# An attention-and-FFN block in float32: queries and keys turned by VectorE and moved through DRAM, with a longer look-ahead

## The chip, the cores and the metric

The kernel runs on one core of a Trainium2 chip. The metric is device time in microseconds (us) of one execution, the median of several runs. A profile is taken from one further execution. TensorE is PE in the profile, VectorE DVE, ScalarE ACT, GpSimd POOL, SyncE SP.

## The reference

One transformer block, B = 8 batches of S = 128 tokens, width 512, everything in float32. Two residual steps:

```python
x = x + attn(cond(x, W[adapter_ids]), wq, wk, wv, wo)          # 32 heads of 16, causal
x = x + ffn(cond2(x, ...), gate, kernel, bias, lora_A, lora_B, ...)

# cond2: attention over a paged cache, 32 query heads, 8 key/value heads of 128
q = rope(rmsnorm(x @ Wq.T, q_norm_w), pos)     # pos = cache_seqlens + arange(128)
k = rope(rmsnorm(x @ Wk.T, k_norm_w), pos);  v = x @ Wv.T
k_all = concat([k_cache[block_table], k])      # 512 cached keys + 128 own keys
v_all = concat([v_cache[block_table], v])
o = softmax(where(valid, q @ k_all.T / sqrt(128), -1e30)) @ v_all
y = o @ Wo.T
# ffn: y @ kernel + bias + two low-rank (LoRA) terms
```

Each key/value head serves four query heads.

## The kernel before

**Phase one** (lines 276 to 798, about the first 220 us) does the first attention, batch by batch, and prepares what the second needs: the cos/sin tables (`tables`, on GpSimd), the gathered adapter weights `cw`, and the merged FFN weights (`merge_loads`, `merge_gates`, `merge_a`, `merge_b`, `merge_w`). x after the first step is kept in SBUF transposed (`x1T`) and in DRAM (`x1_kept`).

**Phase two** is a loop over 64 units, `u = 0 .. 64`. A unit is one key/value head with its four query heads (`g`) and one batch (`b`). Units run in pairs: two neighbouring heads of the same batch, whose cached keys and values lie beside each other and are gathered together. Batches run inside pairs of heads, so that the last pair of heads is units 48 to 63. What pass `u` of the loop issues, in program order:

- `scores(u)`: for each of four heads, one matmul of the head's queries `qT` (the stationary operand) against 512 cached keys `kT`, one against 128 own keys `kTo`; a VectorE step (line 902) that adds the mask and takes the row maximum; an exponential and a division on ScalarE. Score buffers in PSUM (`p_sc`) are two, so the third head waits until the first head's VectorE step is done. Between the heads, `between(r)` issues the query projection of the next unit (`q_matmul`, 4 x 128x512). At the third head `pair_keys(u)` stands.
- After the heads, `q_turn` (rotary embedding of the next unit's queries: three VectorE multiplications, one GpSimd addition, squares on ScalarE), then four VectorE transposes of the probabilities (line 883) and 16 transfers `pT<-fl` on SP's queue, which exchange 32-row blocks so that whole 128x128 transposes result. `pT` is used in the next pass.
- the next unit's key/value projection (`kv_matmul`, `kv_turn`);
- `values(u - 1)`: probabilities of the unit before times values (`op`, line 963), copied to `oT` by VectorE;
- `norms(u + 1)`: the RMS norm factors (power on GpSimd, line 244);
- `queries(u + 1)`: four TensorE transposes of the turned queries `qa` (line 254), evicted to `qT` by ScalarE;
- `out_proj(u - 1)`: `yp` (line 982), added to `y_acc[b]` by VectorE (line 989);
- `own_keys(u + 1)`: one TensorE transpose of the own keys (line 271), evicted to `kTo`.

The cached keys of units 0 to 3 are turned by TensorE (`keys`, line 263). From unit 4 on `turn_keys` turns the keys of a pair in 32x32 blocks by VectorE (line 840), and 16 transfers `kT<-flk` (`move_keys`, line 853), eight in each of two passes, put the blocks in their places inside SBUF. All of these, the weight loads (`load_qkv`, `load_wo`) and the FFN's loads stand in order on SP's queue; the gathers stand on GpSimd's.

The FFN of a batch (`ffn_flip`, `ffn_lora`, `ffn`) runs one pass after the batch's last output projection: passes 51, 53, ... 63, and 64 for the last batch, which has an order of its own (`flips_last`, `out_proj_turned`).

`tile_a` is one ring of twelve 128x512 buffers shared by both phases (`cw`, `la`, `lb`, `sq`, `qa`, `qb`, `qT`, `oT` and others). Tables `ca`, `sa` for all batches lie in SBUF throughout. The order of the work is written out by hand (`tc.manual_schedule()`): each engine takes its instructions in program order.

Of the kernel before, what the change touches and what calls it, by code (L numbers as in the profile page):

```python
# [19 lines left out]
P = 128  # L20
# [21 lines left out]
def block_kernel(  # L42
# [47 lines left out]
    def tile_a(shape, name):  # L90
        return both.tile(shape, F32, tag="a", name=name, bufs=12)
# [18 lines left out]
    ca = [one([P, B, D2], F32, f"ca_{n}") for n in range(2)]  # L110
    sa = [one([P, B, D2], F32, f"sa_{n}") for n in range(2)]
# [11 lines left out]

    weights = {}

    def load_qkv(g):
        wq = wpool.tile([P, KC, REP * D2], F32, tag="wq", name=f"wq_{g}")
        wkv = wpool.tile([P, KC, 2 * D2], F32, tag="wkv", name=f"wkv_{g}")
        e = slice(g * REP * D2, (g + 1) * REP * D2)
        nc.sync.dma_start(out=wq[:], in_=wq2[:, e].rearrange("(c p) e -> p c e", p=P))  # L130
        nc.sync.dma_start(out=wkv[:], in_=wkv2[:, g, :].rearrange("(c p) e -> p c e", p=P))
        weights[g] = [wq, wkv]

    def load_wo(g):
        wo = wpool.tile([P, REP, DM], F32, tag="wo", name=f"wo_{g}")
        e = slice(g * REP * D2, (g + 1) * REP * D2)
        nc.sync.dma_start(out=wo[:], in_=wo2[e, :].rearrange("(r p) o -> p r o", p=P))
        weights[g].append(wo)
# [46 lines left out]
    def q_turn(u):  # L185

        b = units[u][1]
        s = st[u]
        qp = s["qp"]

        def table(t, cols):
            return t[:, b, cols].unsqueeze(1).to_broadcast([P, REP, cols.stop - cols.start])
# [6 lines left out]
        def turn():  # L199
            nc.vector.tensor_tensor(qa[:], qp[:], table(ca[0], slice(0, D2)), ALU.mult)  # L200
            nc.vector.tensor_tensor(qb[:, :, lo], qp[:, :, hi], table(sa[0], lo), ALU.mult)
            nc.vector.tensor_tensor(qb[:, :, hi], qp[:, :, lo], table(sa[0], hi), ALU.mult)
# [18 lines left out]
    def kv_turn(u):  # L221

        b = units[u][1]
        s = st[u]
        kp, ss = s["kp"], s["ss"]
        junk = both.tile([P, D2], F32, tag="junk", name=f"junk_{u}", bufs=1)
        nc.scalar.activation(junk[:], kp[:, :D2], AF.Square, accum_out=ss[:, REP:])
        vo = both.tile([P, D2], F32, tag="vo", name=f"vo_{u}", bufs=3)
        nc.scalar.copy(vo[:], kp[:, D2:])
        ka = both.tile([P, D2], F32, tag="ka", name=f"ka_{u}")  # L230
        kb = both.tile([P, D2], F32, tag="kb", name=f"kb_{u}")
        nc.vector.tensor_tensor(ka[:], kp[:, :D2], ca[1][:, b, :], ALU.mult)
        nc.vector.tensor_tensor(kb[:, lo], kp[:, hi], sa[1][:, b, lo], ALU.mult)
        nc.vector.tensor_tensor(kb[:, hi], kp[:, lo], sa[1][:, b, hi], ALU.mult)
# [3 lines left out]
    def norms(u):  # L238
# [6 lines left out]
        nq = both.tile([P, REP], F32, tag="nq", name=f"nq_{u}", bufs=3)  # L245
# [3 lines left out]

    def queries(u):  # L250
        s = st[u]
        tp = p_tp.tile([P, REP, S], F32, tag="tp", name=f"qTp_{u}")
        for r in range(REP):
            nc.tensor.transpose(tp[:, r, :], s["qa"][:, r, :], ident[:])  # L254
        s["qT"] = tile_a([P, REP, S], f"qT_{u}")
        nc.scalar.copy(s["qT"][:], tp[:])  # L256

    def keys(u):

        s = st[u]  # L260
        tp = p_tp.tile([P, NBLK, P], F32, tag="tp", name=f"kgTp_{u}")
        for c in range(NBLK):
            nc.tensor.transpose(tp[:, c, :], cached(u, "kg", c), ident[:])
        kT = tile_a([P, NBLK * 4, 32], f"kT_{u}")
        nc.scalar.copy(kT[:].rearrange("p k j -> p (k j)"), tp[:].rearrange("p c k -> p (c k)"))
        s["kT"] = kT[:]

    def own_keys(u):
        s = st[u]
        tp = p_tp.tile([P, S], F32, tag="tp", name=f"kTp_{u}")  # L270
        nc.tensor.transpose(tp[:], s["ka"][:], ident[:])
        s["kTo"] = both.tile([P, S], F32, tag="kTo", name=f"kTo_{u}")
        nc.scalar.copy(s["kTo"][:], tp[:])  # L273


    with (
# [69 lines left out]
        ahead = both.tile([P, 4, P], I32, tag="a", name="ahead", bufs=12)  # L346
# [62 lines left out]

        def tables(n):  # L410
            for here, there in ((lo, hi), (hi, lo)):
                w_here = wn[n][:, here].unsqueeze(1).to_broadcast([P, B, HALF])
                w_there = wn[n][:, there].unsqueeze(1).to_broadcast([P, B, HALF])
                nc.gpsimd.tensor_tensor(ca[n][:, :, here], trig["cos"], w_here, ALU.mult)
                nc.gpsimd.tensor_tensor(sa[n][:, :, here], trig["sin"], w_there, ALU.mult)
            nc.gpsimd.tensor_scalar(sa[n][:, :, lo], sa[n][:, :, lo], -1.0, None, ALU.mult)
# [3 lines left out]
        def merge_loads():  # L420
# [7 lines left out]
            for key, src in (("las", lora_as), ("lbs", lora_bs)):  # L428
                merge[key] = tile_a([RANK, DM], key)
# [8 lines left out]
        def merge_gates():  # L438
# [5 lines left out]
            gs = [tile_a([P, 2, B * RANK], f"gs_{n}") for n in range(2)]  # L444
# [256 lines left out]
        for k in range(2 * B + 1):  # L701
# [4 lines left out]
            if hb == 0:  # L706
# [11 lines left out]
                if k == 2 * B:  # L718
                    queries(0)
# [27 lines left out]
            else:  # L747
# [36 lines left out]
                elif b == 2:  # L784
                    tables(1)
                    nc.gpsimd.memset(minus_half[:], -0.5)
# [8 lines left out]
        keys(0)  # L795
        own_keys(0)
# [37 lines left out]
    def turn_keys(n):  # L834


        flk = p2.tile([P, 4, NBLK, 2, 32], F32, tag="flk", name=f"flk_{n}", bufs=1)
        for h, half in enumerate(pairs[n]["kg"]):
            for m in range(2):
                nc.vector.transpose(  # L840
                    flk[:, :, 2 * h : 2 * h + 2, m, :].rearrange("p b c i -> p c b i"),
                    half[:, :, m, :],
                )
        pairs[n]["flk"] = flk
        kT = p2.tile([P, NBLK, 4, 2, 32], F32, tag="kT2", name=f"kT2_{n}")
        pairs[n]["kT"] = kT
        for m in range(2):
            st[2 * n + m]["kT"] = kT[:, :, :, m, :].rearrange("p c a i -> p (c a) i")

    def move_keys(n, a):  # L850

        for b in range(4):
            nc.sync.dma_start(
# [348 lines left out]
```

## Time and profile before

| | us |
|---|---|
| median of 3 runs | 1420.79 (1420.76 to 1423.76) |
| the profiled execution, its time | 1423.96 |
| the profiled execution, its span | 1421.1 |
| granted TensorE clock over the span | 0.997 of full |

| stretch, us from the start of the span | PE busy | DVE busy | ACT busy | POOL busy | DMA share |
|---|---|---|---|---|---|
| 14.78 to 220.69 (phase one) | 197.47 | 137.01 | 104.65 | 109.92 | 0.33 |
| 220.69 to 277.78 (units 0 to 2) | 53.55 | 34.65 | 27.37 | 23.23 | 0.40 |
| 277.78 to 1379.67 (units 3 to 62) | 1100.13 | 738.79 | 512.23 | 423.00 | 0.48 |
| 1379.67 to 1421.10 (end) | 34.20 | 11.63 | 9.81 | 1.26 | 0.15 |

A float32 matmul appears as two matmul records. The ends of matmuls are modelled, so that neighbouring records overlap; the distance from start to start is the better measure of what one costs. "Idle before" in a row is the time in which the engine had nothing to do before this instruction, and the name behind the arrow is what ended it. A `DMA_DIRECT2D` row on SPq is the issue of transfers, not their landing.

### The profile page before, as it was taken

The numbers are of one execution on the slowest core, as the hardware profiler recorded it, in microseconds if no ns is written. First come the engines' busy times: TensorE is split into PE (matmuls) and PEld (weight loads), VectorE is DVE, ScalarE is ACT, GpSimd is POOL, SyncE is SP. The second block draws the span as 40 slices with busy tenths as digits, with TensorE's granted clock in tenths as the row PEclk, the third lists the DMA queues.
The fourth block names the chain that finished last, engine by engine and source line by source line (L and its number), as shares of the span: only waits on it lengthen the run. The fifth ranks groups of instructions, "written<-read, shape, count | busy, mean of one in ns | idle before, by whom it ended". The sixth has DMA issues, their size and how long they took to land.

```text
span 1421.1 us, 20290 instructions
## 1 busy us (share of the span) xinstructions
PE 1391.5 (98%) x6244; PEld 898.5 (63%) x6244; DVE 931.8 (66%) x2266; ACT 655.9 (46%) x1520; POOL 568.2 (40%) x553
## 2 busy tenths in 40 slices
PE   6999989999999999999999999999999999999998
PEld 6877755566666666666666666666666665666555
DVE  5777846566666666666666666666666665666651
ACT  3555535444444444444444444444444444344431
POOL 5774342433333333333333333333333433343220
PEclk9999999999999999999999999999999999999999
DMA  6255013444444565444445654444456544444440
GB/s 198 75 164 183 31 37 104 129 117 118 119 115 119 161 193 151 119 119 119 119 119 159 196 148 119 118 119 119 121 160 192 152 117 136 131 111 112 115 111 30
DMA packets 156202, 180.26 MB, mean 127 GB/s; under 512 B 92416, under 2 KB 97792, under 8 KB 156096
## 3 DMA queue, kind: packets, MB, share of 16 engines
q1 hardware_dynamic: 140544, 134.39, 34.0%
q0 software_dynamic: 15552, 44.58, 10.8%
q8 instruction: 50, 0.82, 0.2%
q14 instruction: 56, 0.46, 0.1%
HBM read 75.83 MB, written 4.72 MB: 57 GB/s over the span
## 4 chain that ended last, share of the span: by engine, by line
PE 93%; DVE 2%; issue 2%; DMA 1%; ACT 1%; POOL 1%; SPq 1%; another core or an unknown queue 0%; DVEq 0%; POOLq 0%; ACTq 0%
PE op L963 19%; PE qp L177 15%; PE sc L889 15%; PE yp L982 15%; PE kvp L217 7%; PE sc L896 4%; PE fp L1044 2%; PE hp L514 2%; PE qTp L254 2%; PE pT1p L638 2%; PE qp L530 2%; PE att L673 2%; PE o L657 1%; PE sc L595 1%; PE kvp L545 1%
## 5 line engine op out<-in xcount | busy, mean ns | idle before, releaser
L902 DVE CUSTOM_DVE_ANT_0 pr<-sc,mask,nq 128x640 f32<-128x640 f32 x256 | 226.0, 884 | 144.2 <-PE sc L896 90.9
L912 ACT ACTIVATE pr<-pr,nm 128x640 f32<-128x640 f32 x256 | 211.8, 827 | 189.3 <-DVE nm L902 102.1
L889 PE MATMUL sc<-kT,qT 128*128 128x512 f32 x512 | 262.0, 593 | 0.0
L177 PE MATMUL qp<-wq,x1T 128*128 128x512 f32 x512 | 251.2, 593 | 0.0
L963 PE MATMUL op<-pT,vg 128*128 128x256 f32 x1024 | 242.0, 379 | 1.6 <-DMA pT<-fl 1.6
L203 POOL TENSOR_TENSOR qa<-qa,qb 128x512 f32<-128x512 f32 x64 | 81.8, 1278 | 375.2 <-DVE sums L879 375.2
L982 PE MATMUL yp<-wo,oT 128*128 128x512 f32 x504 | 229.2, 598 | 2.0 <-DVE oT L971 2.0
L963 PEld LDWEIGHTS op<-pT,vg 128*128 128x128 f32 x1024 | 193.9, 190 | 27.8 <-DVE sums L879 1.8
L880 ACT ACTIVATE pr<-pr,sums 128x640 f32<-128x640 f32 x256 | 208.4, 814 | 0.0
L883 DVE STREAM_TRANSPOSE fl<-pr 128x640 f32<-128x640 f32 x252 | 189.2, 808 | 0.0
L896 PEld LDWEIGHTS sc<-kTo,qT 128*128 128x128 f32 x512 | 96.4, 190 | 124.4 <-issue 119.2
L982 PEld LDWEIGHTS yp<-wo,oT 128*128 128x128 f32 x504 | 91.4, 191 | 95.1 <-issue 91.5
L160 POOL DMA_INDIRECT kg<-in_k_cache_dram,idx_kv x128 | 131.6, 1029 | 35.3 <-issue 34.8
L160 POOL DMA_INDIRECT vg<-in_v_cache_dram,idx_kv x128 | 128.6, 1005 | 37.8 <-issue 33.6
L889 PEld LDWEIGHTS sc<-kT,qT 128*128 128x128 f32 x512 | 87.7, 191 | 80.2 <-issue 77.8
L256 ACT COPY qT<-qTp 128x512 f32<-128x512 f32 x64 | 37.5, 586 | 205.3 <-PE qTp L254 204.7
L217 PEld LDWEIGHTS kvp<-wkv,x1T 128*128 128x128 f32 x512 | 97.3, 190 | 40.5 <-issue 30.1
L217 PE MATMUL kvp<-wkv,x1T 128*128 128x256 f32 x512 | 121.0, 379 | 0.0
L244 POOL TENSOR_TENSOR rs<-ss,minus_half 128x5 f32<-128x5 f32 x64 | 76.5, 1196 | 83.1 <-DVE ss L242 82.2
L177 PEld LDWEIGHTS qp<-wq,x1T 128*128 128x128 f32 x512 | 82.8, 191 | 31.5 <-issue 31.5
L896 PE MATMUL sc<-kTo,qT 128*128 128x128 f32 x512 | 99.2, 275 | 0.0
L273 ACT COPY kTo<-kTp 128x128 f32<-128x128 f32 x64 | 17.1, 267 | 166.4 <-issue 115.2
(155 smaller groups left out, 1701.1 us busy)
## 6 DMA issues: line engine op xcount, KB each, us to landing
pT<-fl SPq DMA_DIRECT2D x1008, 80.0 KB
kT<-flk SPq DMA_DIRECT2D x480, 32.0 KB
wq<-in_wq_dram SPq DMA_DIRECT2D x8, 1024.0 KB
wo<-in_wo_dram SPq DMA_DIRECT2D x8, 1024.0 KB
wkv<-in_wkv_dram SPq DMA_DIRECT2D x8, 512.0 KB
kg<-in_k_cache_dram,idx_kv POOLq DMA_INDIRECT x128
vg<-in_v_cache_dram,idx_kv POOLq DMA_INDIRECT x128
res<-x_kept SPq DMA_DIRECT2D x8, 256.0 KB
```

What stands on the lines that cost most here:

```text
L160: nc.gpsimd.indirect_dma_start(out=dst[:, c].rearrange("p n d -> p (n d)"), out_offset=None, in_=src, in_offset=bass.IndirectOffsetOnAxis( ...
L177: nc.tensor.matmul(s["qp"][:].rearrange("p h d -> p (h d)"), x1T[b][:, c, :], weights[g][0][:, c, :], start=(c == 0), stop=(c == KC - 1),)
L203: nc.gpsimd.tensor_tensor(qa[:], qa[:], qb[:], ALU.add)
L217: nc.tensor.matmul(s["kp"][:], x1T[b][:, c, :], weights[g][1][:, c, :], start=(c == 0), stop=(c == KC - 1))
L880: nc.scalar.activation(prs[r][:], prs[r][:], AF.Copy, scale=sums[:, r : r + 1])
L883: nc.vector.transpose(s["flips"][:, :, :, r, :].rearrange("p b c j -> p c b j"), prs[r][:])
L889: nc.tensor.matmul(sc[:, : NBLK * P].rearrange("p (k j) -> p k j", j=32), s["qT"][:, r, :], s["kT"], start=True, stop=True,)
L896: nc.tensor.matmul(sc[:, NBLK * P : NK], s["qT"][:, r, :], s["kTo"][:], start=True, stop=True)
L902: nc.vector.tensor_tensor_reduce(out=pr[:], in0=sc[:, :NK], in1=mask[:], scale=s["nq"][:, r : r + 1], scalar=3.0e38, op0=ALU.add, op1=ALU.min,
L912: nc.scalar.activation(pr[:], pr[:], AF.Exp, bias=nm[:, r : r + 1], scale=-1.0, accum_out=sums[:, r : r + 1],)
L963: nc.tensor.matmul(ops[h][:, : 2 * S], cached(u, "vg", c) if c < NBLK else s["vo"][:], s["pT"][:, :, c, 2 * h : 2 * h + 2, :].rearrange("p ...
L982: nc.tensor.matmul(yp[:], s["oT"][:, r, :], weights[g][2][:, r, :], start=(r == 0), stop=(r == REP - 1))
```

## The change

Seven things change together.

1. *Turning.* From unit 8 on neither queries nor own keys are transposed by TensorE. `turn_ahead(v)` turns both of a unit in 32x32 blocks by VectorE, the queries of a pair's two units interleaved element by element (`flq[..., m]`). Units 1 to 7 keep TensorE transposes (`flip`, `flip_own`), and TensorE turns the cached keys of units 0 to 7 (`flip_keys`); `turn_keys` starts at pass 5 with pair 4.
2. *Moving.* The 16 SBUF-to-SBUF transfers of a pair are replaced by five stores to DRAM in an even pass (`keys_out`) and eight loads in the odd pass after it (`keys_in`), which carry cached keys, own keys and queries.
3. *Reading.* Queries are read by the score matmuls from a tile of the pair with a step of two elements, keys from a tile in the order block, unit, chunk.
4. *Look-ahead.* The projections run 2, then 3, then 4 units ahead: pass 0 projects units 1 and 2, passes 1 to 3 one unit each, passes 4 and 5 two each, every later pass unit `u + 4`. Passes 60 to 62 have none.
5. *Tables.* The cos/sin tables go to DRAM once (`tab_kept`) and are loaded for each pair (`load_tab`).
6. *Queues.* The weights of heads 2 to 7 are issued on GpSimd's queue, the query and key/value weights three passes earlier.
7. *FFNs.* Batches 0 to 2 keep passes 51, 53, 55; batches 3 to 7 stand at passes 60 to 64.

Buffers: the `tile_a` ring shrinks from twelve to nine, some small tiles get more, and `las`, `lbs`, `gs` get tiles of their own.

```diff
 def tile_a(shape, name):
-    return both.tile(shape, F32, tag="a", name=name, bufs=12)
+    return both.tile(shape, F32, tag="a", name=name, bufs=9)
...
+def load_tab(n):
+    if n < N // 2:
+        tabs[n] = both.tile([P, 4, D2], F32, tag="tab", name=f"tab_{n}")
+        nc.sync.dma_start(out=tabs[n][:], in_=tab_kept[n % B])
...
-    nc.sync.dma_start(out=wq[:], in_=wq2[:, e].rearrange("(c p) e -> p c e", p=P))
+    queue = nc.sync if g < 2 else nc.gpsimd
+    queue.dma_start(out=wq[:], in_=wq2[:, e].rearrange("(c p) e -> p c e", p=P))
...
 def turn_keys(n):
-    flk = p2.tile([P, 4, NBLK, 2, 32], F32, tag="flk", name=f"flk_{n}", bufs=1)
+    flk = p2.tile([P, 4, 2, NBLK + 1, 32], F32, tag="flk", name=f"flk_{n}", bufs=1)
     # four nc.vector.transpose, 128x256 each, as before
+    flq = p2.tile([P, 4, REP, 32, 2], F32, tag="flq", name=f"flq_{n}", bufs=1)
+    pairs[n]["fl"] = [flk, flq]
+    turned_tiles(n)
+
+def turned_tiles(n):
+    kT = p2.tile([P, 4, 2, NBLK + 1, 32], F32, tag="kT2", name=f"kT2_{n}")
+    qT = p2.tile([P, REP, 4, 32, 2], F32, tag="qT2", name=f"qT2_{n}")
+    pairs[n]["to"] = [kT, qT]
+    for m in range(2) if n else (1,):
+        s = st[2 * n + m]
+        s["kT"] = kT[:, :, m, :NBLK].rearrange("p a c i -> p c a i")
+        s["qT"] = [qT[:, r].rearrange("p a i m -> p (a i) m")[:, :, m] for r in range(REP)]
+        s["kTo"] = kT[:, :, m, NBLK]
...
+def turn_ahead(v):
+    (flk, flq), m = pairs[v // 2]["fl"], v % 2
+    nc.vector.transpose(
+        flq[:, :, :, :, m].rearrange("p b r i -> p r b i"),
+        st[v]["qa"][:].rearrange("p r d -> p (r d)"),
+    )
+    nc.vector.transpose(flk[:, :, m, NBLK], st[v]["ka"][:])
+
+def keys_out(n):
+    flk, flq = pairs[n]["fl"]
+    kk = dram.tile([P, 4, 320], F32, tag="kk", name=f"k_kept_{n}", bufs=2)
+    kq = dram.tile([32, 4 * REP, 4, 64], F32, tag="kq", name=f"q_kept_{n}", bufs=2)
+    nc.sync.dma_start(out=kk[:], in_=flk[:].rearrange("p b m c i -> p b (m c i)"))
+    for a in range(4):
+        nc.sync.dma_start(
+            out=kq[:, :, a],
+            in_=flq[32 * a : 32 * a + 32].rearrange("p b r i m -> p (b r) (i m)"),
+        )
+    pairs[n]["dr"] = [kk, kq]
+
+def keys_in(n):
+    kT, qT = pairs[n]["to"]
+    kk, kq = pairs[n]["dr"]
     for b in range(4):
+        part = slice(32 * b, 32 * b + 32)
+        nc.sync.dma_start(
+            out=kT[part].rearrange("p a m c i -> p a (m c i)"),
+            in_=kk[:].rearrange("(a j) b x -> j b a x", j=32)[:, b],
+        )
+        nc.sync.dma_start(
+            out=qT[part].rearrange("p r a i m -> p (r a i m)"),
+            in_=kq[:, REP * b : REP * b + REP].rearrange("j r a x -> j (r a x)"),
+        )
 def pair_keys(u):
-    if u == 2:
-        turn_keys(u)
-    if 1 < u < N - 2:
-        for a in range(u % 2 * 2, u % 2 * 2 + 2):
-            move_keys(u // 2 + 1, a)
+    if 5 < u < N - 2:
+        if u % 2 == 0:
+            turn_ahead(u + 3)
+            keys_out(u // 2 + 1)
+        else:
+            keys_in(u // 2 + 1)
...
-pending = []
+ffn_at = {N - 13 + 2 * b: b for b in range(3)}
+ffn_at.update({N - 7 + b: b for b in range(3, B)})
 for u in range(N + 1):
+    if u < 4:
+        ahead = [u + 2] if u else [1, 2]
+    elif u < 6:
+        ahead = [2 * u - 2, 2 * u - 1]
+    else:
+        ahead = [u + 4] if u + 4 < N else []
+    early = {0: [1], 1: [2, 3], 2: [4], 3: [5], 4: [6], 5: [7]}.get(u, [])
...
-        norms(u + 1)
-        queries(u + 1)
-        for v in {0: (1,), 1: (2, 3)}.get(u, ()):
-            keys(v)
-        if u > 2 and u % 2 and u // 2 + 2 < N // 2:
-            turn_keys(u // 2 + 2)
+    if ahead:
+        norms(ahead[0])
+    for v in {0: [1], 1: [2, 3], 2: [4, 5], 4: [6, 7]}.get(u, []):
+        flip_keys(v)
+    for v in early:
+        flip(v)
+    if u > 4 and u % 2 and u // 2 + 2 < N // 2:
+        turn_keys(u // 2 + 2)
+        turn_ahead(u + 3)
...
-    if nxt:
-        own_keys(u + 1)
+    for v in early:
+        flip_own(v)
+    if len(ahead) > 1:
+        project(ahead[1])
+        norms(ahead[1])
+    if u in (0, 1, 3, 4) or u > 4 and u % 2:
+        load_tab({0: 2, 1: 3, 3: 4, 4: 5}.get(u, (u + 7) // 2))
```

`project(v)` issues `q_matmul`, `q_turn`, `kv_matmul` and `kv_turn` of one unit in a row. In phase one `load_tab(0)` and `load_tab(1)` follow the store of the tables on SP's queue.

## The prediction

> **What bounds the kernel now.** I read the page first, then the chain of waits for two loop passes in mid-kernel (u = 26 and 27), then the timeline of all engines over the same stretch, then the SP queue, then TensorE's own waits.
>
> The page: the last column that matters is PE's share of the span.
>
> ```profile
> span 1421.1 us, 20290 instructions
> PE 1391.5 (98%) x6244; PEld 898.5 (63%) x6244; DVE 931.8 (66%) x2266; ACT 655.9 (46%) x1520; POOL 568.2 (40%) x553
> ```
>
> A busy PE need not be PE at its peak, so the chain of waits decides (start us, us, what):
>
> ```profile
> 713.58 1.73 PE kvp L217 x8
> 715.31 4.32 PE op L963 x20
> 719.63 0.44 PE qTp L254 x4
> 720.06 3.44 PE yp L982 x8
> 723.50 0.11 PE kTp L271
> 723.61 0.86 PE sc L889 x2
> 724.47 0.22 PE sc L896 x2
> ```
>
> There is no wait in it: each piece starts where the last ended. A pass is 4 heads x (0.86 + 0.22) + qp 3.44 + kvp 1.73 + op 4.32 + qTp 0.44 + yp 3.44 + kTp 0.11 = 17.8 us, and the chain shows passes of 17.8 us. TensorE work that leaves a pass shortens it, until another engine's loop is longer.
>
> VectorE at the turn of a pass, and the SP queue (rows of the timeline):
>
> ```profile
> 722.01 1.42 DVE L840 STREAM_TRANSPOSE flk<-kg 128x256 f32<-128x256 f32 x4
> 723.54 0.69 DVE L989 TENSOR_TENSOR y<-yp,y 128x512 f32<-128x512 f32 x1
> 724.14 0.55 DVE L874 TENSOR_SCALAR mask<-place,lens_f 128x640 f32<-128x640 f32 x1
> 724.83 0.88 DVE L902 CUSTOM_DVE_ANT_0 pr<-sc,mask,nq 128x640 f32<-128x640 f32 x1
> 726.47 1.02 PE L889 MATMUL sc<-kT,qT 128*128 128x512 f32 x2
> ```
>
> ```profile
> 710.38 5.15 SPq L853 DMA_DIRECT2D kT<-flk  x8
> 718.03 10.89 SPq L936 DMA_DIRECT2D pT<-fl  x16
> 729.03 5.15 SPq L853 DMA_DIRECT2D kT<-flk  x8
> ```
>
> VectorE runs without a break from 722.01 into the new pass. The third head's score matmul (726.47) needs a score buffer that the first head's softmax step (L902, 724.83) gives back after some 0.95 us; 0.7 us are spare. SP issues for 16 of 17.8 us, 0.6 us a transfer. The last pT piece lands about 2.1 us after its issue (the chain near the end: "DMA pT<-fl" 2.12), at 731.0, and op wants it at 732.9.
>
> TensorE's few losses lie at the ends:
>
> ```profile
> PE yp L982 <- DVE oT L971: 2.0, 1, 2.0
> PE op L963 <- DMA pT<-fl: 1.6, 1, 1.6
> ```
>
> and in pass u = 2, where VectorE turns the first cached keys in mid-scores (windows, one pass each; PEclk third from the end):
>
> ```profile
> 705.66:723.45 17.79, 17.79 (x68) 11.23 (x67) 13.08 (x34) 8.42 (x18) 7.10 (x8) 1.00 0.44 118
> 255.89:277.78 21.89, 19.89 (x68) 11.77 (x67) 11.49 (x32) 8.79 (x19) 11.00 (x12) 0.92 0.43 122
> ```
>
> **The change part by part**, summed against this profiled execution (1423.96 us, its span 1421.1).
>
> *TensorE transposes of 56 units go.* 0.44 + 0.11 = 0.55 us each: -30.8 us. The evictions on ScalarE go too (0.59 + 0.27 a unit); it is 46% busy, nothing. Cached keys of units 4 to 7 are now turned by TensorE: 16 x 0.11 = +1.8.
>
> *VectorE takes them.* One 128x512 and one 128x128 transpose a unit. The trace has 4 of 128x640 in 3.00 us (0.75 each) and 4 of 128x256 in 1.42 (0.34): by that slope 0.61 and 0.2, 0.82 a unit. The 128x512 one writes every second element, of which there is no row: bounds are the same price and double it; I take the same. In even passes it stands between the third and fourth head, where the rows before L902 are 0.97 us idle: hidden, and what exceeds the gap has another 0.7 us before qa. In odd passes it follows the four flk transposes, ahead of y and mask. In the frame of the rows above PE's new pass starts at 722.90; VectorE ends flk at 723.35, the new transposes at 724.17, y at 724.8, mask at 725.3; L902 from 725.3 gives the buffer back at 726.25, while PE is there at 725.92. 0.33 us of stall; counted for 27 odd passes, +8.9. The bounds: nothing if the y addition is less late than I have it, 0.95 each if the strided write doubles (+26).
>
> *The move through DRAM.* Per pair of units SP issued 16 kT pieces; now it is 5 stores, 8 loads and a table load, 14, at 0.6 us: SP has no more to do than before. The stores wait for VectorE's transposes in the even pass (done some 6.2 us into it); behind them on SP stands pT, whose source is ready 12.3 us in: 5 x 0.6 fits, even 5 x 1.38 (w_eff's issue, the longest row of a plain load) is 0.8 us late only. The loads wait for stores issued a pass earlier; they end about 10.3 us into the odd pass, 1.2 MB at the 200 to 240 GB/s of busy microseconds take 5 to 6, and they are needed at 17.2. Hidden; if they came 3 us late it would be 28 x 3 us. Traffic rises from 118 GB/s to some 190. A rule speaks against it: "DMA: Bandwidth & Descriptors" in the Trainium skill (Specifications) has transfers under 512 B pay a read-modify-write, and 2048 runs a pair are 256 B, now into DRAM. The row: kT's 256-B runs, alone on the engines from 712 to 717, moved 231 KB in a summed share of 1.0 us x 16, so 18 ns a run. By the row the stores take 2.3 us of 16 engines a pair, at four times that 9 us of 34.5: the mean share goes to 0.6 or to 0.8, off the path either way. I take nothing.
>
> *Queries read with a step of two.* Each qT stationary is now every second element of a tile shared by two units. No row has a strided weight load. Contiguous ones follow each other at 0.11 us (two in 0.30), which the 0.11 us of a 128-column pass (L896, 0.22 for two) just covers. At half rate four loads in the kTo passes and one between heads 0 and 1 stick out by 0.107 each, 0.53 us a unit. The skill's "SBUF — State Buffer" (Door 1, SBUF cachelines) says that a 16-byte line needs two hits for full bandwidth; a step of 8 bytes has two. By the rule the cost is 0, by the pessimistic reading 63 x 0.53 = 33 us. I take 0.
>
> *Look-ahead in steps.* Passes 0, 4 and 5 project a second unit at their end, 5.17 us of PE work that passes 60 to 62 no longer have: no sum. But its VectorE, ScalarE and GpSimd tail (qa 0.69, 0.41, 0.41, squares 0.60, pow 1.20, mask 0.55) now stands ahead of the next L902: about 3.8 us from the last projection matmul to L902, 4.75 to its buffer, against 3.0 us of PE work: 1.75 us stall, three times, +5.3. Nothing to 3.5 each: in the u = 2 window a 2-us gap also dropped the clock to 0.92. Several PSUM evictions in a row in passes 1 to 4: +1.
>
> *Pass 2 turns nothing in mid-scores:* 21.89 - 17.79 = -4.1.
>
> *Weights on GpSimd's queue.* 18 issues at 0.8 us (wq_sb and wo_sb there: 0.83, 0.80). Queued behind are the next gathers and the qa addition, which has a whole pass to spare now. Nothing; without that cover 14 us spread over 12 passes.
>
> *Phase one.* Nine buffers in place of twelve make three lb loads wait for the last cw (155.4), so w_eff and gc leave behind them: gc lands near 163, where gs ran from 161.6 to 164.5 (mostly blocked). +0.5, at most 5. The table's 2-MB store and two loads stand on SP between xs (101) and the next xs (122.9): hidden.
>
> *Tail.* Passes 60 to 62 have 5.2 us FFN in place of 5.2 us projection, but the projection lay ahead of op and the FFN lies behind it. pT of unit 59 lands 12.3 + 10.1 + 2.1 = 24.5 us after its pass began; op is reached after 17.2 + 4.3 + 0.44 = 22.0. 2.5 lost, and an estimated 1.9 over the next three; today's 1.6 and some 0.4 go. +2.4.
>
> Sum: -30.8 + 1.8 + 8.9 + 5.3 + 1.0 - 4.1 + 0.5 + 2.4 = **-15.0**. The profiled execution would be 1409; the median of the three runs lies 3.2 us lower, so **1406**.
>
> **The rivals.** (1) *Nothing sticks out:* VectorE's odd-pass delay and the projection stalls are absorbed. For it: my slack is 0.3 us in a chain of ten instructions. Against: VectorE is back to back there today. -15.0 - 8.9 - 3 = 1394. (2) *The strided stationary operand:* weight loads at half rate. -15 + 33: **1439, slower**. It decides above 0.05 us per load (15 us over 63 x 5 loads), a pitch of 0.16 for 0.11. Against it is the line rule; for it only that no row shows one. (3) *pT comes late:* its slack falls from 1.9 to about 1.4 us as the pass shrinks, and the engines carry 60% more. Landing 0.25 us beyond it in every pass eats all (60 x 0.25 = 15): 1421; a microsecond, 1466. Against: stores and loads are issued outside pT's own 10 us. (4) *VectorE's strided transpose at double price:* -15 + 17 = 1423. That the transposes don't leave TensorE can be excluded from the diff.
>
> **How the numbers follow.** A measurement here can tell about 0.2% (2.8 us) from no change. My forecast 0.60; (1) 0.14; (2) 0.08; (3) 0.12, half of it near no change or a little under; (4) 0.06. Faster: 0.60 + 0.14, with a little of (3) and (4): 0.75. Same: 0.06. Slower: 0.19. The range from 1393, the end of (1), to 1427, past (4) and the mild half of (3).
>
> **What would show it.** PE instructions 6244 - 280 + 16 = 5980. Passes of 17.25 us when even, near 17.6 when odd, with TensorE waiting for L902 ahead of the third head. In the windows of passes 4, 5 and 6 a stall of about 2 us. Weight loads of the scores still at 190 ns, two in 0.30. pT's wait on PE only at pass 60 and later. I am wrong if op waits for pT in mid-kernel, if score weight loads lengthen, or if odd passes are as long as even ones.

## The result, and the profile after

The changed kernel takes 1457.78 us (median of 6 runs, 1452.28 to 1466.37) against 1420.78 us (1418.77 to 1423.76) of the kernel before on the same chip: a ratio of 1.0266 [1.0232, 1.03], slower by 2.7%. The forecast was 1406 us and faster. The instruction counts came as foreseen (PE 5980); what was not foreseen is in the first lines of the page: TensorE is no longer busy throughout.

```profile
span 1454.8 us, 19520 instructions
PE 1381.6 (95%) x5980; PEld 880.1 (60%) x5980; DVE 967.1 (66%) x2370; ACT 604.9 (42%) x1412; POOL 571.7 (39%) x571
...
PE 75%; DVE 7%; DMA 6%; SPq 4%; issue 3%; POOL 2%; ACT 2%; another core or an unknown queue 0%; ACTq 0%; DVEq 0%; POOLq 0%
```

The last line is the share of the chain that ended last. Before, 93% of it was PE; now a quarter of it is other engines and transfers. PE's busy time fell by 10 us and the span rose by 34.

First the undisturbed passes, because they are what the prediction was mostly about. Two neighbouring passes (windows of the changed kernel; after the length come PE, PEld, DVE, ACT, POOL, then clock, DMA share, GB/s):

```profile
877.62:895.27 17.65, 17.55 (x61) 10.71 (x60) 13.42 (x36) 7.36 (x16) 6.75 (x7) 1.00 0.63 172
895.27:912.56 17.29, 17.29 (x61) 10.80 (x60) 12.51 (x34) 7.47 (x16) 7.02 (x8) 1.00 0.70 175
```

17.29 and 17.65 us where there were 17.79: the forecast had 17.25 and 17.6. The loss must lie elsewhere. Summed by passes, each from its first score matmul in the timeline to the next one's:

| stretch | before, us | after, us | difference | forecast |
|---|---|---|---|---|
| up to the first score matmul | 220.62 | 225.68 | +5.1 | +0.5 |
| passes 0 to 6 | 128.59 | 152.56 | +24.0 | +19.5 |
| passes 7 to 59 | 971.82 | 978.96 | +7.1 | -30.8 |
| pass 60 to the end | 100.07 | 97.60 | -2.5 | -4.2 |

(The 15.5 us of projections and 10.5 us of FFNs that move from one stretch to another are in both last columns.) Of the 48.7 us between forecast and result, 37.9 lie in passes 7 to 59, and there in eleven of 53 passes: 11, 12, 16, 17, 27, 28, 32, 33, 43, 48 and 49, with 18.9 to 24.3 us each. In each of them GpSimd issues weights of heads 2 to 7, some 3.5 us into the pass (in program order they stand at the end of the pass before); of the passes in which it does so only the twelfth, 44, is not long (17.61). Pass 27, from the chain of waits of the changed kernel (start, us, what):

```profile
744.10 0.96 POOL kg L168
745.06 0.00 issue
745.06 7.40 DMA wq<-in_wq_dram
752.46 1.64 issue
754.10 4.55 PE op L1050 x20
```

and the 5-us windows around it:

```profile
740.00:745.00 5.00, 5.00 (x16) 2.48 (x15) 3.48 (x9) 1.10 (x3) 3.90 (x5) 1.00 0.67 184
745.00:750.00 5.00, 5.00 (x18) 2.80 (x17) 2.50 (x8) 4.39 (x9) 1.66 (x3) 1.00 0.88 266
750.00:755.00 5.00, 2.04 (x10) 1.52 (x9) 2.04 (x6) 2.03 (x6) 1.26 (x1) 1.00 1.07 260
```

The timeline has GpSimd issue wq at 745.06 and wkv at 745.87; SP has issued the sixteenth pT piece by 746.9, and the eight key and query loads follow. The DMA engines are full from 750 (share 1.07), TensorE is busy 2.04 of 5 us, and op starts at 754.1 instead of about 751. op doesn't read wq: it reads pT. SP's own rows show that pT was late. Its last query load waited for a pT transfer (a row of SP's waits, then two of its timeline):

```profile
SPq L936 <- DMA pT<-fl: 2.8, 1, 2.8
750.59 0.32 SPq L932 DMA_DIRECT2D kT<-k_kept  x1
753.68 0.30 SPq L936 DMA_DIRECT2D qT<-q_kept  x1
```

That transfer landed at about 753.7, some seven microseconds after SP had issued the last pT piece, and op began 0.4 us later. In the kernel before, the weights were issued on SP behind the last pT piece of a pass (wq at 478.88, when SP had just issued the sixteenth). The waits of TensorE over the whole run show who is late (line, what ended the wait by the profile, us in total, times, longest):

```profile
PE op L1050 <- issue: 13.8, 5, 3.7
PE op L1050 <- DMA qT<-q_kept: 8.7, 2, 4.7
...
PE op L1050 <- DMA tab<-tab_kept: 6.6, 3, 2.3
```

In these three rows alone op waits for 29 us in ten places; before it was 1.6 us in one. The names behind the arrows are inferred: op reads neither qT nor tab. What op reads of the transfers is pT and gathered values, and the experiments below decide between causes.

Not all of the loss is waiting. Passes 17, 33 and 43, with waits of 4.0, 4.7 and 3.5 us, had a granted clock of 0.93, 0.86 and 0.92, and TensorE was busy for 1.9 to 2.4 us more than in a quiet pass. Pass 33 as a window:

```profile
853.27:877.62 24.35, 19.65 (x62) 12.32 (x61) 12.79 (x34) 7.54 (x16) 7.67 (x8) 0.86 0.67 178
```

### The profile page after: what moved, and what is told of

It is laid out like the page before. It is cut to its first block, busy times and chain, and to the rows that moved or that the text cites. A ratio compares the mean times of both kernels' runs of the same rounds, so it can differ in the third digit from the quotient of the medians.

```text
span 1454.8 us, 19520 instructions
## 1 busy us (share of the span) xinstructions
PE 1381.6 (95%) x5980; PEld 880.1 (60%) x5980; DVE 967.1 (66%) x2370; ACT 604.9 (42%) x1412; POOL 571.7 (39%) x571
## 4 chain that ended last, share of the span: by engine, by line
PE 75%; DVE 7%; DMA 6%; SPq 4%; issue 3%; POOL 2%; ACT 2%; another core or an unknown queue 0%; ACTq 0%; DVEq 0%; POOLq 0%
PE op L1050 17%; PE qp L185 12%; PE sc L972 11%; PE yp L1069 11%; PE kvp L225 6%; SPq L1023 3%; PE sc L979 3%; PE hp L534 2%; PE fp L1131 2%; PE pT1p L658 2%; DMA wq<-in_wq_dram 2%; PE att L693 1%; PE qp L550 1%; DVE fl L966 1%; DMA tab<-tab_kept 1%
## 5 line engine op out<-in xcount | busy, mean ns | idle before, releaser
L1050 PE MATMUL op<-pT,vg 128*128 128x256 f32 x1024 | 247.2, 385 | 33.2 <-issue 13.8
L972 PE MATMUL sc<-kT,qT 128*128 128x512 f32 x512 | 265.9, 601 | 9.3 <-DVE nm L989 6.8
L966 DVE STREAM_TRANSPOSE fl<-pr 128x640 f32<-128x640 f32 x252 | 189.6, 810 | 34.4 <-issue 14.7
L979 PEld LDWEIGHTS sc<-kT,qT 128*128 128x128 f32 x504 | 99.0, 197 | 118.1 <-issue 118.1
L972 PEld LDWEIGHTS sc<-kT,qT 128*128 128x128 f32 x512 | 92.9, 196 | 103.3 <-issue 81.0
L168 POOL DMA_INDIRECT kg<-in_k_cache_dram,idx_kv x128 | 124.9, 976 | 35.8 <-issue 35.0
L168 POOL DMA_INDIRECT vg<-in_v_cache_dram,idx_kv x128 | 124.8, 975 | 35.5 <-issue 32.1
L979 PE MATMUL sc<-kT,qT 128*128 128x128 f32 x504 | 98.5, 277 | 0.0
L242 POOL TENSOR_TENSOR ka<-ka,kb 128x128 f32<-128x128 f32 x64 | 29.3, 458 | 159.2 <-DVE kb L241 157.3
L649 POOL TENSOR_TENSOR pr<-pr,sums 128x1024 f32<-128x1024 f32 x32 | 60.1, 1898 | 77.3 <-DVE sums L648 64.2
```

Source lines behind the costliest of these rows:

```text
L168: nc.gpsimd.indirect_dma_start(out=dst[:, c].rearrange("p n d -> p (n d)"), out_offset=None, in_=src, in_offset=bass.IndirectOffsetOnAxis( ...
L966: nc.vector.transpose(s["flips"][:, :, :, r, :].rearrange("p b c j -> p c b j"), prs[r][:])
L972: nc.tensor.matmul(sc[:, : NBLK * P].rearrange("p (c a j) -> p c a j", c=NBLK, j=32), s["qT"][r], s["kT"], start=True, stop=True,)
L979: nc.tensor.matmul(sc[:, NBLK * P : NK].rearrange("p (a j) -> p a j", j=32), s["qT"][r], s["kTo"], start=True, stop=True,)
L1050: nc.tensor.matmul(ops[h][:, : 2 * S], cached(u, "vg", c) if c < NBLK else s["vo"][:], s["pT"][:, :, c, 2 * h : 2 * h + 2, :].rearrange("p ...
```

## The experiments

The kernels run in four groups, each on one chip with runs of the kernel before beside it; ratios are against these. After each run I give the length of passes 7 to 59 of its profiled execution, since that is where the 38 us are (before 971.8, after 979.0).

### Is it the queue of the weights?

```diff
# after_sp_weights: the changed kernel, all weights on SP's queue
-        queue = nc.sync if g < 2 else nc.gpsimd
+        queue = nc.sync
```

> The changed kernel with all weights issued on SP's queue again, at the same points of the loop. Theory A (place in the queue): a weight load on GpSimd's queue shares the DMA engines packet by packet with the last pT pieces of the same pass, so op waits; on SP's queue it stands behind them. Passes 11, 12, 16, 17, 27, 28, 32, 33, 43, 44, 48, 49 lose their extra 2 to 7 us (about 38 us in sum): 1420 us, within 3. Theory B (volume): the pass carries too many bytes since keys and queries go through DRAM, whatever the queue: pT still comes late in those passes, only a few us are won, 1450 or more. Theory C (GpSimd itself is late for its own work because it issues weights): as A in time, but then op's wait would end with GpSimd's qa or pow, not with a transfer.

1435.78 us, ratio 1.0108 [1.0091, 1.0125]; passes 7 to 59 take 953.3. So 22 of the 37 us come back with the queue; the rest does not, and theory A's 1420 is not reached. The places that still lose are mostly odd passes (11, 17, 27, 33, 43, 49: 18.3 to 21.0 us; also pass 18 with 19.0), and the wait is another:

```profile
PE sc L972 <- DMA pT<-fl: 6.3, 3, 3.5
...
PE sc L972 <- DMA qT<-q_kept: 2.4, 2, 1.6
PE sc L972 <- DMA kT<-k_kept: 1.9, 1, 1.9
```

Now it is mostly the score matmuls that wait: on SP the weights stand ahead of the loads of keys and queries, which the new data path needs by the end of that pass (the scores read no pT; that name is inferred). The kernel before had less behind its weights: eight transfers of 32 KB a pass, where there are now eight of 128 and 160 KB in every second pass.

```diff
# before_pool_weights: the kernel before, weights of heads 2 to 7 on GpSimd's queue, nothing else
-        nc.sync.dma_start(out=wq[:], ...)
+        queue = nc.sync if g < 2 else nc.gpsimd
+        queue.dma_start(out=wq[:], ...)
...
```

> The kernel before with only its weights of heads 2 to 7 moved to GpSimd's queue, at their old points in the loop; nothing goes through DRAM. Theory A: op waits in the passes after a load here too; slack is 0.5 us larger per pass and there are no key loads, so 20 to 35 us are lost: 1441 to 1456. Theory B (volume): traffic is as light as it was, so nothing is lost: 1421, within 3.

1442.33 us, ratio 1.0148 [1.0132, 1.0165]: 20 us slower, with none of the traffic through DRAM. Passes 7 to 59 grow from 971.8 to 990.9. One of its hit passes, from the chain of waits:

```profile
497.10 0.04 issue
497.15 7.70 DMA pT<-fl
504.84 1.05 issue
```

A pT piece issued at 497.15 lands after 7.70 us; GpSimd had issued wq at 496.23 and wkv at 497.03. An undisturbed last piece took 2.1. This one edit is enough to make the old kernel slower than it was, by about half of what the changed kernel loses in these passes.

### Is it the place in the pass?

```diff
# after_pool_early: GpSimd's queue kept, issued behind the own keys' rotation; wo a pass later
     kv_turn(ahead[0])
     after[1]()
+    # load_qkv(g) at the same u as in the change; load_wo(g) one u later
...
-    # at the end of the pass
```

> The changed kernel with its weights still on GpSimd's queue, but issued some 13 us into the pass, right behind the ka addition and ahead of the gathers, instead of at the end of the pass (wo one pass later). Same queue, same bytes; the 1.5 MB should have drained when the last pT pieces are issued 22 us into the pass. Theory A in its narrow form (what counts is that the load meets the last pT pieces): about 1422 us. If any load on GpSimd's queue disturbs pT, or if volume counts (B): still 1445 to 1458.

1429.19 us (1422.69 to 1430.79), ratio 1.0056 [1.0039, 1.0073]; passes 7 to 59 take 948.7. Some 29 us come back with the same queue and the same volume, so the place decides. What is left is short waits of op:

```profile
PE op L1050 <- DMA pT<-fl: 8.7, 7, 1.5
```

Why this place is better is argued, not shown: issued 13 us into the pass, the weights run beside the first pT pieces, whose lateness the 10 us of issue that follow can absorb; issued at the end of the pass they meet the last pieces, which by the prediction's working have 1.4 us.

### Is it the volume?

```diff
# after_quarter: one of four 128-row chunks per weight transfer, used four times
+        k = KC if g < 2 else 1
-        queue.dma_start(out=wq[:], in_=wq2[:, e]...)
+        queue.dma_start(out=wq[:, :k], in_=wq2[: k * P, e]...)
...
```

> The changed kernel with its 18 weight transfers on GpSimd's queue at the same places, but each fetches only the first of its four 128-row chunks, and the projections of heads 2 to 7 use this chunk four times: the output of these heads is not the reference's, the work of every engine is the same. Theory A (pT and keys share the DMA engines with the bytes of the weights): the loss in passes 11, 12, 16, 17, 27, 28, 32, 33, 43, 48 and 49 falls from 38 us to under 10: 1420 to 1428. Rival B (an issue on GpSimd's queue itself holds something up, 0.8 us each and what is behind it): 1450 and more, as now.

1414.61 us, ratio 0.9987 [0.9979, 0.9995]. Passes 7 to 59 take 940.8 us, where the forecast, which charged nothing for the weights, had 971.8 - 30.8 = 941.0. The output of these heads is not the reference's, but instructions, queue and places are the same: the bytes (and the packets that carry them) are the cost, not the issue. TensorE's waits for transfers in the loop are nearly gone (the first of these rows is pass 60):

```profile
PE op L1059 <- DMA pT<-fl: 1.2, 1, 1.2
...
PE op L1059 <- DMA kT<-k_kept: 1.0, 2, 0.6
```

With the two runs before it this settles the cause of the 38 us: the bytes of the weights, on a queue beside SP's, at this place in the pass. How much of it the smaller slack and the key and query loads add to the 19 us of the old kernel, no run separates. "DMA: Bandwidth & Descriptors" in the Trainium skill (Queues, rings and completion order) says that each DMA engine takes turns, packet by packet, between the queues that have work for it. The runs fit it, without showing the single packets: beside a weight load on another queue a pT piece of 80 KB took 7.70 us (above), where it took 2.1 with the weights behind it on SP's queue.

### The gate values behind w_eff

```diff
# after_sp_gc: as after_sp_weights, the four gc loads first in merge_loads
 def merge_loads():
+    merge["gc"] = ...; 4 x nc.sync.dma_start(out=merge["gc"]..., in_=gate...)
...
-    # the same loads behind w_eff, las and lbs
```

> The changed kernel with weights on SP's queue, and in phase one the four gc loads issued first in merge_loads instead of last, so that they don't stand behind lb, w_eff and the small loads. VectorE waited 6.1 us for gc, and phase one ended 5.1 us later than before, 3.9 of it at that place. If that wait is the cause: 3 to 4 us faster than the version with weights on SP alone (1416), and the first score matmul at about 222 in place of 225.7. If VectorE's wait is covered by something else: no difference.

1432.24 us, ratio 1.0066 [1.005, 1.0083]: 3.5 us less than without it, by medians of runs that scatter by 4 and 8 us. VectorE's rows of `gs` (it is computed from gc, the gate values, four loads of 4 KB), first of the changed kernel, then of this one:

```profile
168.74 1.43 DVE L467 TENSOR_TENSOR gs<-gc,sel 128x256 f32<-128x256 f32 x4 [6.08 <-DMA gc<-in_gate_dram]
```

```profile
162.68 2.96 DVE L467 TENSOR_TENSOR gs<-gc,sel 128x256 f32<-128x256 f32 x4
```

The 6.08 us of idle VectorE are gone. The first score matmul moves from 224.3 to 222.3 us; in the last two kernels that ran side by side with and without this edit it stood at 215.3 and 218.3. So gc is 2 to 3 us of phase one.

### The odd passes and the weights again

```diff
# w2_gc: gc first; wq and wo early on GpSimd's queue; wkv on SP at the end of an odd pass
+        g = (u + 3) // (2 * B) * 2 + 2
+        if (u + 3) % (2 * B) == 2 * B - 2 and g < NKV:
+            load_kv(g)
+            load_kv(g + 1)
-        if u == first:
+        if u == first + 1:
             ffn_loads(0)
```

> The changed kernel with three moves of transfers and no other edit: the gate values gc are issued first among the FFN-merge loads; wq and wo of heads 2 to 7 stay on GpSimd's queue, but are issued right behind the own keys' rotation, some 13 us into the pass, while pT is still being issued; wkv goes to SP's queue behind the pT of an odd pass, so that what waits behind it are stores and not loads; the first FFN's loads leave a pass later. Theory A (a bulk load costs only where it meets transfers that cannot catch up, and its size at that moment matters): the run with all weights early still lost about 1.5 us in each of passes 11, 12, 27, 43, 44 and 1.9 in pass 49; half of its volume is taken from there, so 4 to 8 us less than that run's 1429, with 3.9 more from gc: 1416 to 1421, passes 11 to 13, 27 to 29 and 43 to 45 within 0.5 us of their neighbours. Rival B (it is the total traffic, not the place): no pass changes, only gc's 3.9: 1425.

1428.1 us (1422.45 to 1429.34), ratio 1.0042 [1.0027, 1.0058]. A miss: pass 11 came down to 17.55, but pass 12 rose to 23.9, pass 28 to 21.9, pass 44 to 22.4, because wkv was now too late itself:

```profile
PE kvp L231 <- DMA wkv<-in_wkv_dram: 8.8, 3, 3.5
```

Waits of 2.4 to 3.5 us made these passes 4.3 to 6.5 us longer: the granted clock over them was 0.86 to 0.92 (a closer look below with w4).

```diff
# w2_gc_mid: as w2_gc; in odd passes the turning moves to the middle of the scores
     else:
         keys_in(u // 2 + 1)
+        if u // 2 + 2 < N // 2:
+            turned_blocks(u // 2 + 2)
+            turn_ahead(u + 3)
...
-    turn_ahead(u + 3)   # behind turn_keys at the end of the pass
```

> The kernel with the rearranged weights and gc, and in addition the turning of queries and own keys for odd passes is moved from the end of the pass, ahead of the y addition and the mask, into the middle of the scores, where the even passes have it. Theory A (the 0.36 us by which every second pass is longer is VectorE arriving late at the first softmax step): the 17.64-us passes become 17.28, 23 of them: 8 us less than the kernel without this edit. Rival B (the scores' middle has no room in odd passes, or pT comes later because VectorE is later): the even passes become shorter and the odd ones longer, 0 us.

1426.15 us, ratio 1.0033 [1.002, 1.0046]. The mechanism holds: the undisturbed even passes from 20 on go from 17.64 to 17.28 or 17.29, and no undisturbed odd pass grows by it. But these are 14 passes and 5 us, not 23 and 8: the other even passes stood at 17.28 to 17.35 already (8 to 16, and 52 to 56, each behind a pass with an FFN), or were set by a load. Over the stretch 7 to 59 only 2.8 us are left (955.5 to 952.7), since passes 17, 18, 27, 28, 44 and 49 lost 3.3 us more to their loads in this run.

```diff
# w2_gc_mid_start: as w2_gc_mid; sums of squares and norms of the second projection left to the next pass
-            for part in q_turn(v):
-                part()
+            turn, squares = q_turn(v)
+            turn()
...
+            deferred.extend([squares, lambda: norms(v)])
...
         if r == 2:
+            while deferred:
+                deferred.pop(0)()
             pair_keys(u)
```

> As the kernel with the turning in the middle of the scores; in addition the sums of squares and the norm factors of the second unit projected in passes 0, 4 and 5 are left to the third head of the next pass, so that VectorE no longer waits for ScalarE and GpSimd ahead of the next pass's mask and first softmax step. Theory A (the long passes 1, 5 and 6 are this chain): pass 1 from 22.2 to about 19 us, pass 5 from 25.4 to 23.5, pass 6 from 21.5 to 18.5: 6 to 8 us less. Rival B (they are long because of the gathers and the evictions of early units): under 2 us.

1418.17 us (17 runs), ratio 0.9977 [0.9968, 0.9985]: 8 us less by the medians and 5.1 by the profiled executions, 4.7 of these in passes 0 to 6. Pass 1 fell from 22.2 to 19.9, passes 5 and 6 together by 2.9. TensorE's wait for the softmax step in passes 0 to 6 is gone; ahead of the edit it read

```profile
PE sc L986 <- DVE nm L1003: 6.5, 3, 2.2
```

which are the three stalls of the forecast, 2.2 us each at most, where it had 1.75.

### The four repairs together, and one step too far

```diff
# w3_gc_mid_start: as w2_gc_mid_start; wkv early on GpSimd's queue, that of the odd head a pass after its wq
+        g = (u + 2) // (2 * B) * 2 + 3
+        if n and (u + 2) % (2 * B) == 2 * B - 2 and g < NKV:
+            load_kv(g)
```

> The kernel with the turning in mid-scores and the deferred norms, but wkv returned to GpSimd's queue at the early place: for the even head beside its wq, for the odd head a pass after its wq. Theory A (what remained of the loss on loads were three waits of the key/value projection for a wkv that came 3.6 us late, in passes 12, 28 and 44, 5 us each with the slower clock behind them): these passes come to 17.3 to 17.5, while passes 11, 27 and 43 go to 18.5 with 1.5 MB beside pT: about 10 us less than 1418, so 1407 to 1411, faster than before by 0.8%. Rival B (the loads take 5 us from the kernel wherever they stand): 1415 to 1418.

1404.14 us (1402.05 to 1409.52) against 1416.29 of the kernel before on this chip: ratio 0.9916 [0.9896, 0.9936]. This is the fastest of the versions. Passes 12, 28 and 44 are at 17.3; what is left of the loads is 1.2 to 2.3 us in passes 11, 13, 27, 34 and 43.

```profile
span 1400.3 us, 19536 instructions
PE 1365.0 (97%) x5980; PEld 874.9 (62%) x5980; DVE 968.9 (69%) x2370; ACT 606.2 (43%) x1412; POOL 571.6 (41%) x571
```

The same 5980 matmul records are now 97% of a span that is 54.5 us shorter than that of the changed kernel (profiled on another chip).

```diff
# w4: as w3_gc_mid_start; wq, wkv and wo issued between the heads, ahead of the qa addition
     if r == REP - 1:
         after[:] = q_turn(ahead[0])
+        # load_qkv, load_kv, load_wo, under the same conditions on u
...
-    # behind kv_turn(ahead[0]); after[1]()
```

> As the kernel with all four repairs, but the weights of heads 2 to 7 are issued another 2 us earlier in the same passes, behind the last query projection matmul and ahead of GpSimd's qa addition, so before the first pT transfer. Theory A (what is left, 1.2 to 2.3 us in passes 11, 13, 27, 34 and 43, is pT pieces at the end of their run still meeting weight bytes): these passes lose under 1 us each, 4 us less than 1404. Rival B (wkv waits there for the key/value projection anyway, and the loads now meet the keys' transfers): 0 us.

1428.57 us, ratio 1.0088 [1.0059, 1.0116]: both theories missed, it is slower by 24 us. The shift was also larger than the 2 us of the expectation: wq left 5.2 us earlier in pass 10 (420.5 for 425.7) and 6.8 earlier in pass 11, since GpSimd no longer stood behind its additions, and wo left 3.6 us into its pass and not 13.3. Pass 10 bears the earlier place (it stays at 17.35, and op of pass 11 waits for nothing). Two kinds of pass don't. In the odd pass 11 GpSimd issues wq at 437.83, in the middle of SP's eight key and query loads (437.14 to 441.8), and the chain of waits has

```profile
438.70 7.78 DMA qT<-q_kept
446.49 0.02 issue
446.50 3.85 DMA pT<-fl
```

A query load of 128 KB takes 7.78 us, what stands behind it is late too, and the scores of pass 12, which read these keys and queries and no pT, wait for 3.3 us. The windows show what such a wait costs beyond itself (clock third from the end):

```profile
440.00:445.00 5.00, 5.00 (x21) 3.73 (x20) 3.76 (x10) 0.74 (x4) 1.44 (x3) 1.00 0.95 281
445.00:450.00 5.00, 2.04 (x5) 0.57 (x3) 2.19 (x7) 0.59 (x1) 3.89 (x5) 0.97 1.06 210
450.00:455.00 5.00, 4.63 (x9) 2.59 (x10) 0.89 (x2) 0.92 (x2) 1.35 (x2) 0.50 0.86 242
455.00:460.00 5.00, 5.00 (x14) 2.32 (x14) 2.98 (x9) 2.90 (x6) 0.00 (x0) 0.84 0.66 166
```

Behind the gap the clock is at 0.50 for 5 us and at 0.84 for the next 5. In passes 11 and 12 together w4 loses 4.8 us against w3 for a wait of 3.3.

The other kind are the even passes 16, 32 and 48, which make 12 of the 24 us: there wo leaves while SP still issues the last pT pieces of the pass before, and op waits, as in the changed kernel. In pass 16 wo is issued at 526.33, and a pT piece behind it takes 7.33 us (a row of the chain of waits, one of the timeline):

```profile
527.30 7.33 DMA pT<-fl
534.90 3.60 PE L1069 MATMUL op<-pT,vg 128*128 128x256 f32 x8 [2.48 <-DMA pT<-fl]
```

### The end

```diff
# w2_gc_mid_start_ffn: as w2_gc_mid_start; FFNs of passes 60 to 62 between the heads
+            elif N - 4 <= u < N - 1:
+                # r == 0: ffn_flip(b); r == 1: ffn_lora(b, ...); r == 2: ffn(b, ...), ffn_loads(b + 1)
```

> As the kernel before it; in addition the FFNs of passes 60 to 62 are issued between the heads of the scores, where the projections of earlier passes stood, in place of the end of the pass. Theory A (pass 60 loses 2.5 us because op is reached before pT has landed, passes 61 and 62 some 1.6 each because ScalarE and VectorE between the heads have nothing of TensorE's beside them): all three come to 17.3 to 17.8 us, 4 to 5 us less. Rival B (the FFN's own chain of evictions stands on TensorE's way between the heads): 0 us or a loss of 3.

1424.89 us, ratio 1.0033 [1.0017, 1.0049], 6.7 us slower than without it. From pass 60 to the end it takes 105.3 us instead of 98.5: rival B, and more than it feared. In the waits of this stretch yp stands for oT for 5.0 us, where it was 1.9 in w3. Op of pass 60 no longer waits for pT (0.5 us, for the scores; 1.9 in w3 for pT), but op of pass 63 waits 2.6 us for it: the shortage moved.

```diff
# w3_tail: as w3_gc_mid_start; FFNs of batches 3 to 5 in passes 57, 59 and 61
-    ffn_at = {N - 13 + 2 * b: b for b in range(3)}
-    ffn_at.update({N - 7 + b: b for b in range(3, B)})
+    ffn_at = {N - 13 + 2 * b: b for b in range(6)}
+    ffn_at.update({N - 7 + b: b for b in range(6, B)})
```

> The kernel with all four repairs (weights early on GpSimd's queue, gc first, turning in mid-scores, norms deferred), and in addition the FFNs of batches 3 to 5 back in passes 57, 59 and 61, so that only passes 60 and 62 have neither projection nor FFN. Theory A (pass 60 loses 2.6 us because nothing of TensorE's stands between the scores and op while pT of a short pass 59 is still landing; a pass 59 with its FFN behind op gives pT 5.2 us more): op of pass 60 waits no longer, 2 to 3 us less over the end. Rival B (the shortage only moves: pass 60 without an FFN is bound by ScalarE and VectorE at about 15 us for 12.1 us of TensorE work, and pass 61's op then meets pT): 0 us or a loss of up to 3.

1409.87 us, ratio 0.9971 [0.996, 0.9982]. From pass 57 to the end 154.7 us against 149.3: 5.4 more. Pass 60 is at 14.7, as rival B had it, but pass 61's op then waits:

```profile
PE op L1069 <- DMA pT<-fl: 5.3, 2, 2.9
```

So the change's place for the FFNs, behind the output projection of passes 60 to 62, is the best of the three tried.

## Why the prediction was wrong

The step that failed is "Weights on GpSimd's queue", with its "Nothing; without that cover 14 us spread over 12 passes". It priced the instruction (0.8 us of issue, and what is queued behind it on GpSimd) and not the megabyte that it starts, and it did not ask what the old place had kept apart. On SP the order of issue kept weights and pT from meeting; taking them off this queue took the order away. The measured term: 40 us in eleven passes of the changed kernel (their excess over undisturbed neighbours; 2 of them, in pass 49, the kernel before has too), 2.3 with a quarter of the bytes, 19 for the move to GpSimd's queue alone in the kernel before. The bound that the prediction named, 14 us "without that cover", was the issue time again. The sentence that "the mean share goes to 0.6 or to 0.8, off the path either way" belongs to the same error: a mean share of 0.63 to 0.73 was measured in most quiet passes, and the engines were at 1.07 where it mattered.

The rival "pT comes late" was the right wait with the wrong cause: it put the lateness on the stores and loads in every pass. In undisturbed passes pT is in time, at 171 to 190 GB/s; it is late only where a weight transfer crosses it, and in pass 60. The prediction did state what would prove it wrong, op waiting for pT in mid-kernel, and that is what came.

What held. Removing TensorE's transposes: passes of 17.29 for 17.79. The VectorE stall of every second pass: 0.36 us measured, 0.33 worked out, and gone when the turning moves to the scores' middle. It falls into the even passes, behind the odd ones that turn, where the prediction named the odd ones; and it is absent in passes 8 to 16 (17.35) and 52 to 56 (17.29), which the prediction did not see. With a quarter of the weights' bytes, passes 7 to 59 came within 0.3 us of the forecast, but that close is in part luck: a pass lost 0.50 us and not 0.55 (2.6 us over 53 passes), and the stall came in 18 passes and not in 27 (2.6 us the other way).

What was mis-sized:
- Phase one, +0.5, at most 5: the mechanism (gc behind w_eff) was right, the size about 2 us. "gc lands near 163" was wrong: the four loads were issued from 159.3 to 162.5, behind 1 MB of w_eff on the same queue, and gs could start only at 168.7. Of the 5.1 us in the table the rest lies between executions. On the chip of the first four experiments the old phase one (before_pool_weights) came to its first score matmul at 222.4 us, the changed one at 223.9 and 224.3, and with gc first at 222.3: there the change costs 1.5 to 1.9 us, and all of it is gc.
- Passes 0 to 6, forecast +19.5, measured +24.0. The three second projections stalled as described (6.5 us for 5.3). Pass 6 took 21.55 us at a granted clock of 0.92; in after_pool_early, behind the same wait of 2.2 us, it took 19.84 at 1.00, so 1.7 us are the clock, a possibility that the prediction named. Of the term "pass 2 turns nothing in mid-scores: -4.1" some 2.9 came (21.89 to 19.85, with 0.88 us of key transposes moved in), but its reason was wrong: VectorE is idle for 4.2 us ahead of the third head in pass 2 of the kernel before and for 4.59 in the changed kernel, so the key turning was not the cause. No run tells what is.
- The end, +2.4 within a forecast of -4.2, measured -2.5: pass 60 as described (20.1 us), passes 61 and 62 at 18.9 for 17.3 of TensorE work.

The rival of the strided stationary operand is nearly void. Weight loads of the scores and VectorE's new transposes in the changed kernel (mean ns behind the busy us):

```profile
L979 PEld LDWEIGHTS sc<-kT,qT 128*128 128x128 f32 x504 | 99.0, 197 | 118.1 <-issue 118.1
...
L909 DVE STREAM_TRANSPOSE flq<-qa 128x512 f32<-128x512 f32 x56 | 38.1, 680 | 0.0
L913 DVE STREAM_TRANSPOSE flk<-ka 128x128 f32<-128x128 f32 x56 | 14.9, 267 | 0.0
```

A weight load with a step of two took 197 ns for the 190 of a contiguous one, and the undisturbed pass is 0.04 us above the forecast. The rule on 16-byte lines in the Trainium skill's "SBUF — State Buffer" (Door 1, SBUF cachelines), by which the prediction set this cost to zero, agrees but for these 7 ns. The transpose that writes every second element took 0.68 us for 0.61 worked out: far from double, which puts rival 4 aside too.

## What to carry to other kernels

A queue is also an order. Before moving a bulk transfer to another queue, list which transfers it will then run beside, how much of each one's slack is left at that moment, and price the bytes by the chain's own row (a 1-MB load, 7.4 us from issue to landing here), not the issue by its 0.8 us. A place for it is where the transfers beside it have issue time left to catch up: a load made its pass 0.7 to 2.3 us longer beside the first pT pieces, and with one exception 1.3 to 7 beside the last ones. Sum the loop by passes after a change: quiet and disturbed passes part at once, and a good forecast of the quiet ones can stand while the total is wrong.

## What was not expected of the hardware

- How narrow the good place is: the same weight loads issued 5 to 10 us earlier in a pass of 17.3 (w4) changed a ratio of 0.9916 into 1.0088.
- A gap of 3.3 us in TensorE's work is followed by a granted clock of 0.50 and then 0.84 over 10 us (w4, pass 12). But the length of the gap alone does not decide: a gap of 3.74 us in pass 11 of the changed kernel is followed by the full clock, as one of 3.35 us is in pass 33 of w4, while the gap of 2.0 us in pass 2 of the kernel before is followed by about 0.5 for 3 us. "TensorE: Matmul & The Clock Gate" in the Trainium skill (Part 1) has half the clock after an idle window of about 3.4 us; these gaps do not part at that length. The gap of pass 11 and the window behind it:

```profile
460.93 1.97 PE L1050 MATMUL op<-pT,vg 128*128 128x256 f32 x8 [3.74 <-issue]
461.00:466.00 5.00, 5.00 (x22) 4.18 (x23) 4.56 (x11) 0.00 (x0) 0.46 (x1) 1.00 0.84 176
```

- Some versions scatter widely between runs: 14 us in six runs of the changed kernel and 13 in six of w4, where the kernel before stays within 2 to 7 in groups of 6 to 27 and the version with a quarter of the weights' bytes within 6 in 20. The cause is not shown.
